# Conv-sequence kernel, second layer: slabs of the forward transform loaded turned by 12 time steps, edge rows taken out of them

## Chip, core and metric

The kernel runs on one core of one Trainium2 chip, in one launch. The metric is the device time of that launch in microseconds (us), as the median of several runs. A profile comes from one execution, with its own time beside it. Engines are called PE (TensorE matmuls), PEld (its weight loads), DVE (VectorE), ACT (ScalarE), POOL (GpSimd) and SP (SyncE, which here only issues DMAs).

## What is computed

The input `x` has shape 4 x 512 x 128 x 64 (batch, time T, nodes, channels), all float32. Layer 0 is a block of a gated recurrence, a convolution along the nodes, a causal convolution in time and a feed-forward part; the change doesn't touch it. Layer 1 splits its input into a moving average over 25 time steps and the rest, and filters the rest in the frequency domain:

```python
left = right = 12            # KERNEL = 25
xpad = concat([first row x left, x, last row x right], axis=time)
c = cumsum(xpad); trend = (c[25:] - c[:-25]) / 25
seasonal = x - trend
xs = rfft(seasonal, axis=time)[:, :128]          # 128 modes
ys = einsum('bmnc,cmk->bknc', xs, w_real + 1j * w_imag)
out = trend + irfft(ys padded to 257, n=512, axis=time)
```

The moving average repeats the first and the last row at the ends. If it wrapped around instead, it would be a circular filter, and the transform of `seasonal` would be one fixed matrix times `x`. The kernel uses that matrix (in `dftv` and `dftd`) and adds a correction that depends on only 24 rows: the first 12 and the last 12 time steps (`dfte` holds its matrix, `HALO` is 12).

## The kernel before

Layer 1 works in `layer1` on two batches at a time. Each pair goes through three stages: `transform` of both batches, `mix`, `invert` of both. So there are two forward transforms in a launch. Layer 0 leaves its result in DRAM as `x4[b]`, time steps by 8192 columns (node and channel).

A slab is all 512 time steps of 512 columns: 128 partitions x 4 blocks of time x 512, 1 MB. There are 16 slabs in a batch. `slab` (L928) loads one with a single DMA from SP into a tile `xin`, tag `big`, of which there are 5 buffers. The weights `w` of the mix use the same 5 buffers (L991), and so do the slabs that `invert` loads again.

`transform` (from L933) takes two slabs at a time, k = 0 and 1; a pair is called a group here, 16 groups in the transform of two batches. In a group, for each k:

- GpSimd issues two DMAs that load 12 rows each, the first and the last time steps, into the tile `edge` (L943, L944; tag `edge`, 2 buffers).
- ACT copies those 24 rows to another place in `edge`, 32 partitions on (L945), since the real and the imaginary part use operands at different partitions.
- DVE forms differences and sums of the blocks of time, `v` (L948) and `u` (L949), and then sums and differences of the halves of `u`, `ev` (L952, two each).

Then PE runs, for both k, the matmuls on `v` (L960), on `ev` (L968) and on `edge` (L977), which accumulate into four PSUM banks, tag a or b in turn. ACT copies the banks to `xf` (L983), the spectrum of the whole batch.

`mix` (L985 on) loads 16 tiles `w` of 1 MB; GpSimd flips the sign of parts of each (L994), PE multiplies (L1001, L1005), and the results go back into `xf`. It starts when `xf` of both batches is there. `invert` forms the inverse transform (L1027 to L1039), loads each slab again together with 6 strips `halo` of 12 rows (L1049, L1052, from SP), adds the moving average on PE (L1055, L1058) and stores `out` (L1062).

The matmuls keep the order in which they are written (`manual_schedule` for PE alone). The order on the other engines is the scheduler's; it puts the loads of later groups ahead of the work of earlier ones as the buffers allow. Each engine runs its instructions, and issues its DMAs, strictly in that order. DMA completions are counted by eight semaphores in turn, so that a DMA waits for the eighth one before it.

Of the kernel before, what the change touches and what calls it, by code (L numbers as in the profile page):

```python
# [10 lines left out]
F32 = mybir.dt.float32  # L11
# [5 lines left out]
P = 128  # L17
T = 512
NF = 128
H = 64  # L20
D = NF * H
NCH = D // P
SL = 512
NS = D // SL
NPR = NCH // 2
NT = T // P
# [4 lines left out]
HALO = KMA // 2  # L31
# [14 lines left out]
def conv_seq_kernel(  # L46
# [27 lines left out]

    layer0(tc, dram, x, xt, vecs, wkvr, wo, wdec, wconv, fbias, w1, fb1, w2, fb2, x4)
    layer1(tc, x4, wri, dftv, dftd, dfte, idfte, idfto, avg, avgh, out)


# [799 lines left out]
def layer1(ctx, tc, x4, wri, dftv, dftd, dfte, idfte, idfto, avg, avgh, out):  # L878
# [7 lines left out]
    nc = tc.nc  # L886
# [4 lines left out]
    dft = ctx.enter_context(tc.tile_pool(name="dft", bufs=1))  # L891
    io = ctx.enter_context(tc.tile_pool(name="io", bufs=2))
# [4 lines left out]
    def load(pool, eng, name, src):  # L897
        t = pool.tile(list(src.shape), F32, name=name)
        eng.dma_start(t, src)
        return t  # L900
# [3 lines left out]
    dfte_sb = load(dft, nc.sync, "dfte_sb", dfte)  # L904
# [5 lines left out]
    def bank(tag):  # L910
        return ps.tile([P, SL], F32, tag=tag, name=tag)


    def by_c(row):
        return row.rearrange("p (a c l) -> p a l c", c=H, l=2)

    def by_n(row):
        return row.rearrange("p (a l c) -> p a l c", c=H, l=2)
# [7 lines left out]
    def slab(b, s):  # L926
        xin = io.tile([P, NT, SL], F32, tag="big", name="xin", bufs=5)
        nc.sync.dma_start(  # L928
            xin, x4[b][:, s * SL : (s + 1) * SL].rearrange("(c p) d -> p c d", p=P)
        )  # L930
        return xin

    def transform(b, xf):  # L933

        for g in range(NS // 2):
            edge = io.tile([P, SL], F32, tag="edge", name="edge")
            uv, ev, pf = [], [], []
            for k in range(2):
                s = 2 * g + k
                c = slice(s * SL, (s + 1) * SL)  # L940
                xin = slab(b, s)
                q = k * H
                nc.gpsimd.dma_start(edge[q : q + HALO, :], x4[b][0:HALO, c])  # L943
                nc.gpsimd.dma_start(edge[q + HALO : q + 2 * HALO, :], x4[b][T - HALO : T, c])  # L944
                nc.scalar.copy(edge[q + 32 : q + 32 + 2 * HALO, :], edge[q : q + 2 * HALO, :])  # L945
                u = io.tile([P, 2, SL], F32, tag="uv0", name="u")
                v = io.tile([P, 2, SL], F32, tag="uv1", name="v")
                nc.vector.tensor_tensor(v, xin[:, 0:2, :], xin[:, 2:4, :], ALU.subtract)  # L948
                nc.vector.tensor_tensor(u, xin[:, 0:2, :], xin[:, 2:4, :], ALU.add)  # L949
                t = io.tile([P, 2, SL], F32, tag="ev", name="ev")  # L950
                for i, op in enumerate((ALU.add, ALU.subtract)):
                    nc.vector.tensor_tensor(t[:, i, :], u[:, 0, :], u[:, 1, :], op)  # L952
                uv.append(v)
                ev.append(t)
                pf.append([bank("ab"[g % 2]), bank("ab"[g % 2])])
            for k in range(2):
                for i in range(2):
                    for r in range(2):
                        h = 1 - r
                        nc.tensor.matmul(  # L960
                            pf[k][r][h * H : (h + 1) * H, :], lhsT=dftd_sb[:, i, r, :], rhs=uv[k][:, i, :],
                            start=(i == 0), stop=False,
                        )
            for k in range(2):
                for i in range(2):
                    for r in range(2):
                        q = r * H + i * H // 2
                        nc.tensor.matmul(  # L968
                            pf[k][r][q : q + H // 2, :], lhsT=dftv_sb[:, i, r, :], rhs=ev[k][:, i, :],
                            start=True, stop=False,  # L970
                        )
            for k in range(2):
                for r in range(2):
                    at = slice(k * H + 32 * r, k * H + 32 * r + 2 * HALO)
                    for h in range(2):
                        hs = slice(h * H, (h + 1) * H)
                        nc.tensor.matmul(  # L977
                            pf[k][r][hs, :], lhsT=dfte_sb[at, hs], rhs=edge[at, :], start=False, stop=True
                        )
            for k in range(2):  # L980
                s = 2 * g + k
                for r in range(2):
                    nc.scalar.copy(by_c(xf[:, r, s * SL : (s + 1) * SL]), by_n(pf[k][r]))  # L983
# [86 lines left out]
    with tc.manual_schedule(engines={nc.tensor.engine}):  # L1070
        for b0 in range(0, B, G):
            xf = spec.tile([P, G, 2, D], F32, tag="xf", name="xf")
            for b in range(G):
                transform(b0 + b, xf[:, b, :, :])
            mix(xf)
            for b in range(G):
                invert(b0 + b, xf[:, b, :, :])


def _constants():  # L1080

    a = np.zeros((T, T))
    for t in range(T):
        for s in range(t - HALO, t + KMA - HALO):
            a[t, min(max(s, 0), T - 1)] += 1.0 / KMA
    around = np.zeros((T, T))
    for t in range(T):
        for s in range(t - HALO, t + KMA - HALO):
            around[t, s % T] += 1.0 / KMA
    k, n = MODES, np.arange(T)  # L1090
    angle = 2.0 * np.pi * ((k[:, None] * n[None, :]) % T) / T
    waves = np.stack([np.cos(angle), -np.sin(angle)])

    dft = waves @ (np.eye(T) - around)
    at = np.concatenate([np.arange(HALO), np.arange(T - HALO, T)])
    edge = (waves @ (around - a))[:, :, at]
    dfte = np.zeros((2, 32, M))
    dfte[0, : 2 * HALO] = edge[0].T
    dfte[1, : 2 * HALO] = np.roll(edge[1], H, axis=0).T
    weight = np.where(k == 0, 1.0, 2.0)[:, None] / T  # L1100
    idft = waves * weight
    idft[1, k == 0] = 0.0
    q = H // 2
    idfte = np.concatenate([idft[r, i : i + q, :P] for i in (0, q) for r in range(2)])
    idfto = np.concatenate([idft[r, H:, : T // 2] for r in range(2)])
    tiles = [slice(i * P, (i + 1) * P) for i in range(NT)]
    avg = np.stack([a[s, s].T for s in tiles], axis=1)
    avgh = np.zeros((NT, 32, P))
    for j, s in enumerate(tiles):
        at = [t for t in range(s.start - HALO, s.start) if t >= 0]  # L1110
        at += [t for t in range(s.stop, s.stop + HALO) if t < T]
        avgh[j, : len(at)] = a[s][:, at].T
    c = {
        "dftv": dft[:, :H, :P].reshape(2, 2, H // 2, P).transpose(3, 1, 0, 2),
        "dftd": dft[:, H:, : T // 2].reshape(2, H, 2, P).transpose(3, 2, 0, 1),
        "dfte": np.concatenate([dfte.reshape(2 * 32, M)] * 2),
        "idfte": idfte,
        "idfto": idfto.reshape(M, 2, P),
        "avg": avg,
        "avgh": avgh.reshape(P, P),  # L1120
    }
    return {n: v.astype(np.float32) for n, v in c.items()}


def _inputs(x, i):
# [22 lines left out]
    for rows, parts in ((MODES, ("w_real", "w_imag")), (IMAG, ("w_imag", "w_real"))):  # L1148
# [16 lines left out]
        "fb2": np.concatenate([i["ffn_b2"]] * 2)[:, None],  # L1165
        "wri": wri.reshape(H, M, 2, 2, M).transpose(1, 0, 2, 3, 4),
        **_constants(),
    }
    return {n: np.ascontiguousarray(v) for n, v in a.items()}
# [17 lines left out]
```

## Time and profile before

| | |
|---|---|
| median of 3 runs | 3746.26 us (3743.07 to 3754.74) |
| the profiled execution | 3747.14 us, its span 3745.2 us |
| busy: PE, DVE, ACT, POOL | 3536.6, 2669.1, 1759.4, 522.6 us |
| DMA | 913.42 MB in 429269 packets, 244 GB/s over the span |
| first transform: first load issued, mix begins | 2757.08, 2891.50 us |
| second transform: third load issued, mix begins | 3246.58, 3376.00 us |

The spans of time are from the start of the profiled span. A line of a timeline gives start, length, engine, source line, operation, output and inputs, the count, and in brackets the idle time of the engine before it with what ended it. A line of the table of stretches gives the length of a stretch, the busy time of PE, PEld, DVE, ACT and POOL in it, the granted clock of PE (1.00 is full), the mean busy share of the core's 16 DMA engines, and what they moved in GB/s. The share can pass 1 a little, since packets overlap.

### The profile page before, as it was taken

The numbers are of one execution on the slowest core, as the hardware profiler recorded it, in microseconds if no ns is written. First come the engines' busy times: TensorE is split into PE (matmuls) and PEld (weight loads), VectorE is DVE, ScalarE is ACT, GpSimd is POOL, SyncE is SP. The second block draws the span as 40 slices with busy tenths as digits, with TensorE's granted clock in tenths as the row PEclk, the third lists the DMA queues.
The fourth block names the chain that finished last, engine by engine and source line by source line (L and its number), as shares of the span: only waits on it lengthen the run. The fifth ranks groups of instructions, "written<-read, shape, count | busy, mean of one in ns | idle before, by whom it ended". The sixth has DMA issues, their size and how long they took to land. (4 is left out here: it accounts for less than half of the span.)

```text
span 3745.2 us, 53017 instructions
## 1 busy us (share of the span) xinstructions
PE 3536.6 (94%) x20041; PEld 1368.8 (37%) x20041; DVE 2669.1 (71%) x3498; ACT 1759.4 (47%) x2299; POOL 522.6 (14%) x782
## 2 busy tenths in 40 slices
PE   9999999999998999999999989999988999989998
PEld 4433322234333223433322233333323843328533
DVE  4445569976776896677789799946667277892677
ACT  0013346655656565565656578868854200142100
POOL 0000012310101121001112122100013000130000
PEclk9999999999999999999999999999999999999999
DMA  9867648787875688788568678645567478993687
GB/s 316 276 206 245 226 163 269 255 280 267 288 263 169 233 279 273 267 292 281 178 231 285 214 248 267 232 152 192 201 233 262 156 235 294 316 322 127 214 285 265
DMA packets 429269, 913.42 MB, mean 244 GB/s; under 512 B 33240, under 2 KB 83672, under 8 KB 424920
## 3 DMA queue, kind: packets, MB, share of 16 engines
q1 hardware_dynamic: 351088, 636.91, 52.4%
q0 software_dynamic: 75776, 271.62, 20.0%
q8 instruction: 160, 2.62, 0.3%
q10 hardware_dynamic: 2152, 1.51, 0.1%
q14 instruction: 93, 0.76, 0.1%
HBM read 641.40 MB, written 268.50 MB: 243 GB/s over the span
## 5 line engine op out<-in xcount | busy, mean ns | idle before, releaser
L744 PE MATMUL p<-mid,w_sb 64*64 64x512 f32 x2048 | 554.8, 599 | 20.2 <-DVE wx L757 20.2
L744 PE MATMUL pb<-mid,w_sb 64*64 64x512 f32 x2048 | 536.7, 599 | 0.0
L736 ACT ACTIVATE mid<-c,fb_sb 128x1024 f32<-128x1024 f32 x256 | 284.6, 1112 | 97.5 <-PE c L731 95.1
L736 ACT ACTIVATE mid<-m,fb_sb 128x1024 f32<-128x1024 f32 x256 | 284.9, 1113 | 93.6 <-PE m L731 92.2
L731 PE MATMUL c<-x,w_sb 64*64 64x512 f32 x2016 | 280.7, 610 | 13.2 <-ACT mid L736 6.9
L731 PE MATMUL m<-x,w_sb 64*64 64x512 f32 x2016 | 283.2, 613 | 6.7 <-ACT ob L776 4.9
L744 PEld LDWEIGHTS p<-mid,w_sb 64*64 64x64 f32 x2048 | 155.5, 135 | 294.8 <-issue 261.6
L408 PE MATMUL a<-xp,wx 128*128 128x512 f32 x512 | 241.7, 615 | 9.1 <-DVE wx L357 8.6
L1032 ACT COPY two<-a 128x512 f32<-128x512 f32 x64 | 37.5, 586 | 428.3 <-PE a L1027 428.3
L1055 PE MATMUL b<-xin,avg_sb 128*128 128x512 f32 x512 | 230.8, 593 | 3.3 <-DVE xin L1061 3.3
L1061 DVE TENSOR_TENSOR xin<-b,pm 128x512 f32<-128x512 f32 x256 | 159.1, 684 | 98.0 <-PE b L1058 83.1
L569 ACT ACTIVATE sq<-x 128x1024 f32<-128x1024 f32 x128 | 135.1, 1055 | 179.4 <-DVE x L566 179.2
L624 DVE SCALAR_TENSOR_TENSOR to<-kd,vec,to 128x510 f32<-128x510 f32 (+1 forms) x272 | 197.2, 745 | 9.9 <-ACT to L620 8.7
L924 DVE COPY xf<-b 128x256 f32<-128x256 f32 x128 | 54.4, 425 | 199.1 <-PE b L1001 179.9
L699 ACT ACTIVATE kd<-kd,vec 128x512 f32<-128x512 f32 x256 | 192.8, 803 | 3.2 <-DVE kd L691 3.2
L251 PE MATMUL st<-x,ones 128*32 128x512 f32 x512 | 173.0, 609 | 12.8 <-DVE x L566 12.8
L624 DVE SCALAR_TENSOR_TENSOR z<-x,vec,z 128x511 f32<-128x511 f32 x240 | 175.9, 745 | 5.3 <-ACT z L620 3.0
L702 DVE TENSOR_TENSOR x<-kd,kx 128x1024 f32<-128x1024 f32 x126 | 154.1, 1223 | 32.6 <-ACT kd L699 32.5
L530 DVE TENSOR_TENSOR x<-a,xp 128x1024 f32<-128x1024 f32 x128 | 156.1, 1220 | 29.1 <-PE a L528 26.9
L528 PE MATMUL a<-rst,wo_sb 64*128 64x512 f32 x512 | 149.2, 657 | 25.1 <-DVE x L530 23.3
L567 POOL DMA_DIRECT2D x<-x x128 | 93.6, 731 | 560.4 <-DVE x L566 544.7
L757 DVE SCALAR_TENSOR_TENSOR x4t<-p,fb_sb,x 128x512 f32<-128x512 f32 x64 | 47.9, 748 | 170.6 <-PE pb L744 168.1
(267 smaller groups left out, 6859.6 us busy)
## 6 DMA issues: line engine op xcount, KB each, us to landing
xp<-in_xt SPq DMA_DIRECT2D x256, 512.0 KB
xin<-x SPq DMA_DIRECT2D x128, 1024.0 KB
kh<-to SPq DMA_DIRECT2D x156, 512.0 KB
x<-x POOLq DMA_DIRECT2D x128, 512.0 KB, 4.6
kx<-x SPq DMA_DIRECT2D x128, 512.0 KB
x<-ob POOLq DMA_DIRECT2D x64, 1024.0 KB, 7.9
out<-xin POOLq DMA_DIRECT2D x64, 1024.0 KB, 6.3
x<-x SPq DMA_DIRECT2D x96, 512.0 KB
```

The lines of the kernel that those rows point to most:

```text
L251: nc.tensor.matmul(st[32 * q : 32 * q + 32, :], lhsT=ones, rhs=src[:, j, :], start=first, stop=last,)
L408: nc.tensor.matmul(pa[:, k, :], lhsT=wq[:, j, k * P : (k + 1) * P], rhs=xp[:, j, :], start=first and j == 0, stop=last and j == 1,)
L528: nc.tensor.matmul(at[:, j, :], lhsT=wo_sb[js, :], rhs=rst[js, :], start=True, stop=True)
L530: nc.vector.tensor_tensor(x1, at, xp, ALU.add)
L624: tap = nc.vector.scalar_tensor_tensor(to[:, j, k:], xr[:, j, : SL - k], vec[:, w, c], to[:, j, k:], ALU.mult, ALU.add)
L699: tc.keep_in_program_order(nc.scalar.activation(d[:, j, :], d[:, j, :], AF.Identity, bias=vec[:, B4, c], scale=vec[:, G4, c]))
L702: nc.vector.tensor_tensor(x3, d, x2, ALU.add)
L731: nc.tensor.matmul(pm[halves[j], h, :], lhsT=w1_sb[halves[h], q * H : (q + 1) * H], rhs=x3[halves[h], j, :], start=True, stop=True,)
L736: nc.scalar.activation(mid, pm, AF.Gelu_apprx_tanh, bias=fb1_sb[:, q : q + 1])
L744: nc.tensor.matmul(sums2[i][j][halves[h], :], lhsT=w2_sb[halves[j], q, :], rhs=mid[halves[j], h, :], start=q == 0, stop=q == 3,)
L1055: nc.tensor.matmul(po[j], lhsT=avg_sb[:, j, :], rhs=xin[:, j, :], start=True, stop=False)
L1061: nc.vector.tensor_tensor(by_n(xin[:, j, :]), by_n(po[j]), by_c(pm[j % 2][:, j // 2, :]), ALU.add)
```

## The change

A new function `shifted_slab` loads the slab turned by 12 time steps: partition p of block c holds time step 128 c + p - 12, modulo 512. It takes three DMAs from SP: 116 rows into partitions 12 to 127 of block 0, the last 12 time steps into partitions 0 to 11 of block 0, and 384 rows into blocks 1 to 3. So partitions 0 to 23 of block 0 hold the 24 edge rows, and GpSimd loads none. ACT copies them from the slab into `edge`: once for k = 0 and twice for k = 1. The fourth place isn't filled; for k = 0 and r = 0 the matmul on the edges reads the slab itself. The matrices are turned to match on the host.

```diff
+    def shifted_slab(b, s):
+        xin = io.tile([P, NT, SL], F32, tag="big", name="xin", bufs=5)
+        c = slice(s * SL, (s + 1) * SL)
+        nc.sync.dma_start(xin[HALO:P, 0, :], x4[b][0 : P - HALO, c])
+        nc.sync.dma_start(xin[0:HALO, 0, :], x4[b][T - HALO : T, c])
+        nc.sync.dma_start(xin[:, 1:NT, :], x4[b][P - HALO : T - HALO, c].rearrange("(c p) d -> p c d", p=P))
+        return xin
...
-                xin = slab(b, s)
-                q = k * H
-                nc.gpsimd.dma_start(edge[q : q + HALO, :], x4[b][0:HALO, c])
-                nc.gpsimd.dma_start(edge[q + HALO : q + 2 * HALO, :], x4[b][T - HALO : T, c])
-                nc.scalar.copy(edge[q + 32 : q + 32 + 2 * HALO, :], edge[q : q + 2 * HALO, :])
+                xin = shifted_slab(b, s)
+                ends = xin[0 : 2 * HALO, 0, :]
+                if k == 0:
+                    first = ends
+                for q in (32,) if k == 0 else (H, H + 32):
+                    nc.scalar.copy(edge[q : q + 2 * HALO, :], ends)
...
-                            pf[k][r][hs, :], lhsT=dfte_sb[at, hs], rhs=edge[at, :], start=False, stop=True
+                            pf[k][r][hs, :], lhsT=dfte_sb[at, hs], rhs=edge[at, :] if k + r else first,
+                            start=False, stop=True,
...
-    at = np.concatenate([np.arange(HALO), np.arange(T - HALO, T)])
+    at = np.concatenate([np.arange(T - HALO, T), np.arange(HALO)])
...
+    dft = np.roll(dft, HALO, axis=2)
```

## Prediction

> **What bounds the kernel now.** Read first the chain of waits in order of time, where it passes through the two forward transforms (times in us from the start of the span, length, what).
>
> ```profile
> 2872.21 1.90 PE a L968 x16
> 2875.39 4.16 DMA w<-in_wri
> 2880.78 5.66 DMA edge<-x
> 2887.82 3.64 ACT xf L983 x7
> ...
> 3354.59 6.57 DMA w<-in_wri
> 3361.19 2.97 issue
> 3365.79 5.15 DMA edge<-x
> 3372.32 3.64 ACT xf L983 x7
> ```
>
> Both transforms end on an edge load, and behind it hangs the mix, which needs all of `xf`. The timeline of GpSimd, ScalarE and TensorE there shows why:
>
> ```profile
> 2870.50 9.79 POOL L994 TENSOR_SCALAR w<-w 128x256 f32<-128x256 f32 x4 [6.62 <-DVE ev L952]
> 2880.24 0.55 POOL L943 DMA_DIRECT2D edge<-x  x1
> ...
> 2886.54 1.25 ACT L945 COPY edge<-edge 24x512 f32<-24x512 f32 x2 [13.83 <-DMA edge<-x]
> ...
> 2879.09 1.92 PE L968 MATMUL b<-ev,dftv_sb 128*32 128x512 f32 x16
> 2886.58 3.24 PE L977 MATMUL b<-edge,dfte_sb 24*64 24x512 f32 x16 [5.56 <-DMA edge<-x]
> 2891.50 1.22 PE L1001 MATMUL b<-xf,w 128*128 128x256 f32 x2 [1.68 <-ACT xf L983]
> ```
>
> The last group's edge loads are issued from GpSimd's queue behind the sign flips of `w` (L994), and TensorE stands 5.56 us. Next the middle of the transform, by the table of stretches (seven us each: busy us of PE, PEld, DVE, ACT, POOL, then granted clock, DMA share, GB/s):
>
> ```profile
> 2770.00:2777.00 7.00, 5.65 (x40) 1.42 (x40) 6.80 (x8) 1.85 (x3) 0.00 (x0) 0.76 1.06 376
> 2805.00:2812.00 7.00, 6.60 (x64) 1.91 (x48) 7.00 (x9) 3.46 (x6) 2.00 (x4) 1.00 1.05 346
> 2847.00:2854.00 7.00, 6.60 (x56) 1.91 (x48) 7.00 (x9) 3.46 (x6) 2.00 (x4) 1.00 0.99 314
> ```
>
> DVE is full, 7.00 of 7.00: a group of two slabs takes its two u, two v and four ev, 2.35 + 2.35 + 2.49 less their overlaps, and comes round every 6.95 us. The DMA engines are nearly full as well: 376 GB/s while the buffers fill, 314 when DVE paces them. Last, the timeline of one group, the queue of SP in it:
>
> ```profile
> 2797.70 2.35 DVE L948 TENSOR_TENSOR v<-xin 128x1024 f32<-128x1024 f32 x2
> 2798.94 0.36 SPq L928 DMA_DIRECT2D xin<-x  x1
> ...
> 2804.50 1.11 PE L977 MATMUL a<-edge,dfte_sb 24*64 24x512 f32 x16
> ...
> 2809.33 2.35 DVE L949 TENSOR_TENSOR u<-xin 128x1024 f32<-128x1024 f32 x2
> ```
>
> The first slab's buffer is free when v has read it (2798.92), and SP refills it at once.
>
> [...] Each transfer leaves a 4-byte packet per engine it used. On SP's queue there are 23,536 in the records of DMA packets; the 1,183 issues other than `halo` in the list of issues, all of 128 partitions, account for 16 each, 18,928; the remaining 4,608 are 384 x 12, so a `halo` load of 12 rows runs on 12 engines. No run shows one of 116 rows. [...] L994 takes 407 ns in the median and 8676 at the longest, in the transform's end.
>
> **The change, part by part.**
>
> The 128 edge loads leave GpSimd's queue (0.50 us each, 64 us of an engine busy 14%). That is worth nothing except at the two ends. There L977 of the last group could start when L968 is done, at 2881.0, and the mix at about 2884.2 in place of 2891.5: 7.3 us. At the second end L968 is done at 3366.0, the mix could start at 3369.2 in place of 3376.0: 6.8. Together **-14 us**. Late next would be nothing: `w` has landed by then.
>
> A slab is now three transfers of 116, 12 and 384 rows of 2 KB. SP issues 64 x 3 in place of 64; at 0.36 us that is 1.1 us a slab, hidden in the 3.5 that a slab has. The bytes of the edges (3.1 MB) go. [...] 116 = 4 x 29 runs on k = 4 engines with 29 rows each, the 12 on twelve with one, the 384 on all with 24. The first four engines carry **29 + 1 + 24 = 54 rows** of each slab, against 32 before; they set when it lands. A row costs, at the 376 GB/s of the full engines, 2048 x 16 / 376 = 87 ns; the shortest packet of 2 KB in the records is 84 ns, and at 346 GB/s it is 95. So a slab takes 54 x 87 = 4.70 us, a group **9.4 us in place of DVE's 6.95**: the bound passes from DVE to four DMA engines. [...]
>
> First transform, from the first issue at 2757.08 to the mix. Now 134.4 us. After: 32 slabs x 4.70 = 150.3; other traffic on those engines at the start, a 1 MB store of `x` (2.8 us per engine) and the 0.56 MB of constants (1.6), 4.4; issue and completion 2.4 (the quickest edge load); from the last landing to the mix 11 (u and v 2.4, L960 3.6, L968 1.9, L977 and the copies of `xf` 3). Sum 168: **+34**. The second: two slabs are loaded early, 30 follow from 3246.58, now 129.4. After: 30 x 4.70 = 141 + two 1 MB stores of `out` 5.6 + 2.4 + 11 = 160: **+31**. In both the 14 us of the ends are already taken off. At 84 ns and without other traffic the sum is +45, at 95 ns +91.
>
> ScalarE copies three times 24x512 in a group, not two: 0.62 us more of an engine busy 3.46 of 7.00; hidden, and if it were not, 32 x 0.62 = 20 us at most. But the copies of group g+2 stand ahead of the `xf` copies of g+1 in its order and now wait for the slabs; at 9.4 us a group these land about when L977 of g+1 ends, which costs 0 to 1 us a group (not added; in the upper end). TensorE does the same matmuls. The one that reads `first` straight from the slab holds its buffer till L977 (2805.2, not 2798.9); DVE needs the refilled one at u of the second next group, 2810.5. That leaves 5.3 us to land where there were 11.5. With 9.4 us a group it leaves over 10, so it costs nothing in the likely case. SP's queue stands longer at that wait; behind it are only slabs and then `w`, whose first is needed 11 us after the last slab.
>
> Nothing else in the kernel is touched. The profiled execution took 3747.1 (span 3745.2), 0.9 over the median of 3746.3. So 3747.1 + 65 = 3812, in terms of the median **3811**.
>
> **Rivals.**
> - Even spread, a gain: the 116 rows go over all sixteen engines, some 8 each, so 33 rows a slab, 2.9 us, and DVE still paces. Then only the two ends remain: -14, 3732. For it: only the 12-row case was seen. [...] an even spread of 12 looks the same, which is the weak point. It decides if a 116-row load puts under 41 rows on its busiest engine (6.95 / 2 / 0.087 = 40, so at most 15 of the 116).
> - The held buffer, no change: an even spread, but 5.3 us to land is too short. From release to release two groups later runs landing L, then 8.6 us (u and v 2.4, L960 and L968 5.5, half of L977 0.7); the pace is (L + 8.6) / 2, above 6.95 once L passes 5.3. A 1 MB store of `out` lands in 6.3 in the median, which gives 7.45, +0.5 x 28 groups = +14 against -14: 3746.
> - The edges were hidden anyway, so nothing changes: against it stand 5.56 us of idle TensorE on the chain.
> - Worse: rows queue on four engines at 95 ns or more, or ScalarE's order adds a us a group: +91 and up, 3840 to 3870.
>
> **How the numbers follow.** Four engines 0.76 (3790 to 3838), worse 0.10, even spread 0.07, held buffer or nothing 0.07. The range 3768 to 3848 takes in the first case whole, with 22 below it, [...] and the lower part of the worse case above it; some 2 in 10 are left out. A measurement here tells 0.3%, 11 us, from no change. Slower 0.86, same 0.07, faster 0.07.
>
> **What would show it.** Right: in the transforms' stretches DVE falls from 7.00 of 7.00 to about 5.2, the DMA share to about (4 x 54 + 12 x 25) / 16 x 87 ns / 4.7 us = 0.6 to 0.65, some 225 GB/s, and DVE and ScalarE wait for `xin`; groups come every 9.1 to 9.7 us; no wait for an edge at the ends. Wrong: groups at 6.95 with DVE full (even spread), or alternating short and long with SP waiting for L977 (held buffer).

## The result and the profile after

| | before | after |
|---|---|---|
| median of 6 runs each | 3743.03 us (3738.35 to 3754.74) | 3843.41 us (3826.54 to 3851.83) |
| ratio, with its 95% interval | | **1.0257 [1.0228, 1.0286]** |
| the profiled execution, its span | 3747.14, 3745.2 us | 3849.67, 3847.9 us |
| first transform, first load issued to mix | 134.4 us | 187.5 us (2764.99 to 2952.54) |
| first mix begins to second mix begins | 484.5 us | 529.6 us (to 3482.14) |
| second mix begins to the end of the span | 369.2 us | 365.7 us |

The kernel is 100 us slower; 3811 was forecast, in a range of 3768 to 3848. In the two profiles the spans differ by 102.7 us. The first transform accounts for 53.1 of it and the stretch from mix to mix, which holds the second transform, for 45.1. The rest, +7.9 ahead of the first load and -3.5 after the second mix began, lies in work that the change doesn't touch; the last section has a likely reason for the -3.5.

The page of the kernel after: its span, the queues of DMA (packets, MB, share) and the chain that ended last.

```profile
span 3847.9 us, 53000 instructions
...
q1 hardware_dynamic: 352112, 636.91, 50.9%
q0 software_dynamic: 71680, 268.46, 19.3%
...
PE 31%; DMA 7%; ACT 3%; issue 3%; DVE 2%; SPq 1%; POOL 0%; ACTq 0%; POOLq 0%; DVEq 0%
DMA xin<-x 6%; PE b L1065 4%; PE p L744 4%; PE b L1011 3%; PE b L1015 3%; PE c L731 3%; PE m L731 3%; PE a L1039 3%; PE b L1068 2%; PE a L1037 1%; PE a L969 1%; DMA halo<-x 1%; ACT z L620 1%; PE m L763 1%; PE c L763 1%
```

The load of a slab now heads the list of what the end waited for, with 6% of the span. SP's queue (q1) holds 1,024 packets more than before (352,112 against 351,088). They are all packets of 4 bytes: 24,560 against 23,536. In the kernel before a load over 128 partitions left 16 of them and one of 12 rows left 12, which is read here as one for each engine that a transfer used; the records don't name engines. There are 16 more for each of 64 slabs. Three transfers on k, 12 and 16 engines leave k + 12 more than the one on 16 did, so **k = 4: the 116 rows run on four engines**.

The chain of waits in the first transform (start, length, what), the kernel after:

```profile
2882.20 15.28 DMA xin<-x
2897.50 12.73 DMA xin<-x
2912.86 6.51 PE a L969 x16
...
2925.47 2.53 SPq L937
2928.05 12.11 DMA xin<-x
2942.75 5.22 PE b L969 x16
2947.97 1.85 PE b L977 x16
```

It goes from load to load. The edge load that stood in it before is gone. DVE's timeline shows the beat of the groups:

```profile
2887.85 1.23 DVE L958 TENSOR_TENSOR u<-xin 128x1024 f32<-128x1024 f32 x1 [3.35 <-DMA xin<-x]
...
2899.69 1.23 DVE L958 TENSOR_TENSOR u<-xin 128x1024 f32<-128x1024 f32 x1 [4.07 <-DMA xin<-x]
...
2910.35 1.23 DVE L958 TENSOR_TENSOR u<-xin 128x1024 f32<-128x1024 f32 x1 [3.62 <-DMA xin<-x]
...
2920.39 1.23 DVE L958 TENSOR_TENSOR u<-xin 128x1024 f32<-128x1024 f32 x1 [3.00 <-DMA xin<-x]
```

DVE stands 3 to 4 us in each group for `xin`, and the groups come 10.0 to 11.8 us apart where they came every 6.95. The table of stretches (length; PE, PEld, DVE, ACT, POOL; granted clock, DMA share, GB/s) for the two transforms after:

```profile
2805.00:2840.00 35.00, 26.93 (x152) 6.68 (x152) 24.77 (x28) 13.24 (x24) 0.00 (x0) 0.86 0.68 202
2840.00:2875.00 35.00, 24.80 (x146) 6.34 (x144) 22.65 (x26) 12.02 (x21) 0.00 (x0) 0.80 0.71 202
2875.00:2910.00 35.00, 25.96 (x180) 7.22 (x176) 21.21 (x24) 13.24 (x23) 0.00 (x0) 0.90 0.68 192
...
3365.00:3400.00 35.00, 30.39 (x192) 8.53 (x190) 25.41 (x30) 13.59 (x24) 0.00 (x0) 0.84 0.69 213
```

DVE is down from full to 21 to 25 of 35 us, and yet the DMA engines are only 0.68 to 0.71 busy in the mean. Neither is full. But a mean over sixteen engines can hide four that are, and the records of DMA packets agree: from 2805 to 2910 us and from 3365 to 3400, 4 or 5 packets are under way at once for 26 to 31% of the time and fewer than 4 for at most 1.4%. The kernel before has 12 or more for 98.7 to 99.9% of its time there (2805 to 2865, 3290 to 3325). Last, the waits (us in total, times, longest):

```profile
ACT edge L954 <- DMA xin<-x: 184.8, 55, 7.3
...
DVE u L958 <- DMA xin<-x: 79.1, 32, 4.3
```

### The profile page after: what moved, and what is told of

Read it like the earlier page. It is cut to its first block, busy times and chain, and to the rows that moved or that the text cites. A ratio compares the mean times of both kernels' runs of the same rounds, so it can differ in the third digit from the quotient of the medians.

```text
span 3847.9 us, 53000 instructions
## 1 busy us (share of the span) xinstructions
PE 3582.1 (93%) x20041; PEld 1378.1 (36%) x20041; DVE 2674.9 (70%) x3498; ACT 1776.7 (46%) x2331; POOL 447.7 (12%) x654
## 3 DMA queue, kind: packets, MB, share of 16 engines
q1 hardware_dynamic: 352112, 636.91, 50.9%
## 5 line engine op out<-in xcount | busy, mean ns | idle before, releaser
L691 DVE TENSOR_TENSOR kd<-kd,rm 128x1024 f32<-128x1024 f32 x128 | 155.9, 1221 | 7.5 <-ACT rm L285 6.0
```

Source lines behind the costliest of these rows:

```text
L691: nc.vector.tensor_tensor(d, d, pair_of(mb), ALU.subtract)
```

## The experiments

Ratios are to the kernel before, on the same chip in the same session (medians of before 3743 to 3746 us); "pace" is the mean distance of two groups on PE, read from the matmuls on `v` over the last seven groups of the first transform and the last twelve of the second.

| run | slab's transfers (rows) | rows on fullest engine | pace, us | median us | ratio [95%] |
|---|---|---|---|---|---|
| before | 512 | 32 | 6.95 | 3743 to 3746 | 1 |
| after | 116, 12, 384, turned by 12 | 54 | 10.0 to 10.5 | 3843.41 | 1.0257 [1.0228, 1.0286] |
| e1_all_copied | as after, no slab held | 54 | 10.5 to 10.7 | 3847.61 | 1.0279 [1.0255, 1.0303] |
| e3_split116 | 116, 12, 384, unturned | 54 | 10.4 to 10.5 | 3873.95 | 1.0348 [1.0327, 1.0368] |
| e6_split118 | 118, 10, 384, unturned | 84 | 14.3 to 14.4 | 3986.98 | 1.0659 [1.0626, 1.0691] |
| e10_cut_112_4 | 112, 4, 12, 384, turned by 12 | 33 | 7.3 to 7.5 | 3743.89 | 0.9994 [0.9981, 1.0006] |
| e2_turn16 | 112, 16, 384, turned by 16 | 32 | 7.5 | 3743.13 | 0.9995 [0.9983, 1.0007] |
| e5_turn16_all_copied | as e2, no slab held | 32 | 7.2 to 7.6 | 3737.97 | 0.9988 [0.9977, 0.9998] |
| e4_split112 | 112, 16, 384, unturned | 32 | 8.1 to 8.3 | 3783.07 | 1.0099 [1.0081, 1.0118] |
| e9_split64 | 64, 64, 384, unturned | 32 | 8.1 to 8.3 | 3792.89 | 1.0132 [1.0115, 1.0149] |
| e7_split128 | 128, 128, 256, unturned | 32 | 6.95 | 3743.57 | 1.0003 [0.9992, 1.0014] |
| e8_copied_edges | 512 | 32 | 6.95 | 3727.02 | 0.9953 [0.9935, 0.9971] |

The unturned splits keep the edge loads of before. The theories: F, the fullest engine sets the pace; H, the slab held for the matmul on the edges does; S, several transfers cost what they cost, whatever their rows.

**e1_all_copied** takes away the held slab alone.

```diff
-                for q in (32,) if k == 0 else (H, H + 32):
+                for q in (k * H, k * H + 32):
...
-                            pf[k][r][hs, :], lhsT=dfte_sb[at, hs], rhs=edge[at, :] if k + r else first,
+                            pf[k][r][hs, :], lhsT=dfte_sb[at, hs], rhs=edge[at, :],
```

> The changed kernel, but all four places of the edge rows are filled by ScalarE (four copies in a group, not three), so that no matmul reads the slab and its buffer is free once v, u and the copies have read it. Theory F (four DMA engines carry 54 rows of each slab): the loads are the same, so 3825 to 3855 us, a group every 10 to 11 us. Rival H (the slab held until L986 leaves too little time for the refill): the time goes back to 3735 to 3775. Rival S (three transfers in place of one, with their issues and semaphores): as F, 3825 to 3855.

Measured 1.0279, with an interval that overlaps the changed kernel's. ScalarE's wait for the slab is what it was (184.8 us before this edit), in the waits of this run:

```profile
ACT edge L954 <- DMA xin<-x: 184.6, 58, 7.7
```

H is out for the changed kernel.

**e2_turn16** keeps all of the change, but turns by 16, so that 112 rows go on sixteen engines (SP's queue holds 353,136 packets, 32 a slab more than before); 32 edge rows take the place of 24, with zero weights for eight of them. `TURN` is 16; the other uses of `HALO` in the loads, copies and matrices of the transform change in the same way.

```diff
-        nc.sync.dma_start(xin[HALO:P, 0, :], x4[b][0 : P - HALO, c])
+        nc.sync.dma_start(xin[TURN:P, 0, :], x4[b][0 : P - TURN, c])
...
-    dft = np.roll(dft, HALO, axis=2)
+    dft = np.roll(dft, TURN, axis=2)
```

> The changed kernel turned by 16 time steps in place of 12: the three transfers have 112, 16 and 384 rows, and 32 partitions of block 0 are the edge operand (8 of them with zero weights). All three divide by 16. F: 7 + 1 + 24 = 32 rows on every engine, as in the kernel before; DVE paces again at 6.95 us a group, and the waits at the two ends are gone: 3725 to 3750. H: the hold of the first slab is still there, so at least half of the loss stays: 3790 or more. S: still three transfers, so 3825 to 3855.

Measured 0.9995: the whole loss is gone. But so are the 14 us that the two ends should have given.

**e3_split116** puts the three transfers alone into the kernel before.

```diff
-                xin = slab(b, s)
+                xin = split_slab(b, s)
...
+        nc.sync.dma_start(xin[0:116, 0, :], x4[b][0:116, c])
+        nc.sync.dma_start(xin[116:P, 0, :], x4[b][116:P, c])
+        nc.sync.dma_start(xin[:, 1:NT, :], x4[b][P:T, c].rearrange("(c p) d -> p c d", p=P))
```

> The kernel before, not turned, with its edge loads, but each slab of the forward transform loaded by three transfers of 116, 12 and 384 rows. F: 54 rows of each slab on four engines, so the transforms slow as in the changed kernel: 3830 to 3865 (the waits for edges at the ends may stay). H: no slab is held, so 3740 to 3755. S: 3830 to 3865.

Measured 1.0348, 9 us above the highest time expected, at the pace of the changed kernel. The three transfers alone make the loss. That it is some 30 us greater fits what stands there beside them: the edge loads, and the waits at the ends, where the mix begins 15.7 and 15.5 us after the last matmuls on `v` (9.8 and 8.2 in the changed kernel). The two ends are 13 of the 30.

**e4_split112** is e3 with 112 in place of 116.

> As the one before, but split into 112, 16 and 384 rows. F: 32 rows on every engine as with one transfer: 3740 to 3760. H: 3740 to 3755. S (three transfers cost, whatever their rows): 3830 to 3865. With the run of 116, 12 and 384 rows beside it, this changes only which engines carry the rows.

Measured 1.0099. Most of e3's loss is gone, and yet 37 us stay with 32 rows on every engine: F does not account for all of it. The table of stretches of this run says where to look (GB/s last):

```profile
2840.00:2875.00 35.00, 31.19 (x222) 8.75 (x226) 29.11 (x33) 13.23 (x24) 8.01 (x16) 0.95 1.07 265
```

All sixteen engines are full now (1.07), at 265 GB/s. Before, they were as full at 314 to 346. So the rows themselves take longer. In the records of DMA packets, rows of 2 KB take 127 to 130 ns in the mean here, 98 in the kernel before.

**e5_turn16_all_copied** is e2 with e1's edit.

> The turned loads by 16 rows (112, 16 and 384 rows, spread evenly over sixteen engines) with all four places of the edge operand copied by ScalarE, so that no matmul on the edges reads the slab and its buffer is free when v and the copies have read it. Theory H for the even case: there the groups come at about 7.2 us, and the slab held until L977 leaves too little time to land; that eats the 14 us of the two ends, and without the hold the time is about 3732 (ratio 0.996). Theory N (a row's place): rows of a 112-row and a 16-row transfer cost more each (112 to 116 ns in the run before, against 97 in the kernel before) with the DMA engines full, so that transfer and not the hold sets the pace: 3740 to 3746 (ratio 0.998 to 1.000), rows again at 110 to 116 ns and the DMA share near 1.00.

Measured 0.9988. The interval leaves out the 0.996 that H gave, and it overlaps e2's: a few us at most belong to the held slab, and whether any do is not settled. Rows take 118 to 120 ns, slow as theory N had them and a little above its 110 to 116; the median lies 2 us below its 3740 to 3746.

**e6_split118** is e3 with 118, to put more rows on fewer engines.

> The kernel before with its edge loads and unturned slabs, the slab loaded as 118, 10 and 384 rows. Theory F (engines used = largest divisor up to 16): 118 = 2 x 59 runs on two engines, 10 on ten, so the busiest two carry 59 + 1 + 24 = 84 rows of a slab, in place of 54 with 116 rows. At the 97 ns a row of the four-engine case a slab takes 8.1 us, a group 16.3 in place of about 10.4 there: 30 groups add about 280 us to the before, some 4025. Every slab leaves 2 + 10 + 16 = 28 completion packets of 4 bytes where an unsplit one leaves 16. Theory S (three transfers cost the same whatever their rows): as with 116 rows, 3874, or as with 112 rows, 3783.

Measured 1.0659. There are 24,304 completion packets of 4 bytes, 12 more a slab than before, as two engines want. DVE's timeline:

```profile
2907.45 1.23 DVE L957 TENSOR_TENSOR u<-xin 128x1024 f32<-128x1024 f32 x1 [5.51 <-DMA xin<-x]
...
2921.49 1.22 DVE L957 TENSOR_TENSOR u<-xin 128x1024 f32<-128x1024 f32 x1 [5.51 <-DMA xin<-x]
...
2935.62 1.23 DVE L957 TENSOR_TENSOR u<-xin 128x1024 f32<-128x1024 f32 x1 [5.54 <-DMA xin<-x]
```

A group every 14.1 us here, 14.3 to 14.4 over the transforms: 2 x 84 rows at 85 ns. The count was right and the price too high: the forecast of +280 took 97 ns, and +243 came. F has passed with a second divisor, and S has failed.

**e7_split128** asks whether e4's 37 us are the price of three DMAs in place of one.

```diff
+        nc.sync.dma_start(xin[:, 0, :], x4[b][0:P, c])
+        nc.sync.dma_start(xin[:, 1, :], x4[b][P : 2 * P, c])
+        nc.sync.dma_start(xin[:, 2:NT, :], x4[b][2 * P : T, c].rearrange("(c p) d -> p c d", p=P))
```

> The kernel before with its edge loads and unturned slabs, the slab loaded by three DMAs of 128, 128 and 256 rows, each over all 128 partitions. It tells apart why 112, 16 and 384 rows, which spread evenly over sixteen engines, still cost 37 us. Theory N (a row's place: a transfer over fewer than 128 partitions gives each engine rows that cost more): nothing is left, 3740 to 3752, rows at about 97 ns as before. Theory L (three DMAs for a slab where eight semaphores count completions in turn, so that fewer slabs are under way, and SP issues three times as much): the 37 us stay, 3775 to 3790, rows as cheap as before or the DMA share below 0.95.

Measured 1.0003, and DVE is full again:

```profile
2830.00:2865.00 35.00, 33.01 (x248) 9.70 (x244) 35.00 (x42) 17.32 (x30) 9.98 (x20) 1.00 0.95 319
```

Here three transfers, with three issues on SP and three turns of the semaphores, cost nothing; each of them goes over all 128 partitions. Rows take 94 ns.

**e9_split64** is e4 with 64 in place of 112; it asks whether two equal pieces cost what 112 and 16 rows do.

> The kernel before with its edge loads, the slab loaded as 64, 64 and 384 rows: all three spread evenly over sixteen engines. It asks why 112, 16 and 384 rows cost 37 us and 128, 128 and 256 nothing. [...] Theory G (any transfer over fewer than 128 partitions makes all rows slow, in it and behind it): as with 112 and 16 rows, three quarters of the rows at 100 to 160 ns, 3775 to 3795.

Measured 1.0132, the same pace as e4, at 258 GB/s:

```profile
2840.00:2875.00 35.00, 29.67 (x194) 8.22 (x196) 29.36 (x34) 14.38 (x26) 7.98 (x16) 0.89 1.06 258
```

In the records 73 to 84% of the rows take 100 to 160 ns and under 10% more than that. The two pieces hold only a quarter of the rows, so those of the 384-row transfer, three quarters of all, are slowed as well. G, which only says what happens, fits.

**e10_cut_112_4** is the changed kernel with its 116-row transfer cut in two.

```diff
-        nc.sync.dma_start(xin[HALO:P, 0, :], x4[b][0 : P - HALO, c])
+        n = P - 16
+        nc.sync.dma_start(xin[HALO : HALO + n, 0, :], x4[b][0:n, c])
+        nc.sync.dma_start(xin[HALO + n : P, 0, :], x4[b][n : P - HALO, c])
```

> The changed kernel with one edit: its transfer of 116 rows is cut into two, 112 rows (7 on each of sixteen engines) and 4 rows (one on each of four), so that a slab is four transfers and the busiest engine carries 7 + 1 + 1 + 24 = 33 rows in place of 54. Everything else of the change stays, the turn by 12 and the slab read by the matmul on the edges too. Theory F (engines used = largest divisor up to 16, and the fullest engine sets the pace): nearly all of the 97 us goes, 3735 to 3755; the rows still cost about 115 ns with the engines full, as with a turn by 16. Theory S (what costs is that a slab is several transfers): 3843 or more. Completion packets a slab: 16 + 4 + 12 + 16 = 48.

Measured 0.9994. Four rows moved into a transfer of their own take away the whole 100 us, though the slab is four transfers now. Completion packets are 25,584, or 32 a slab more than before, as expected. Its two transforms in the table of stretches:

```profile
2830.00:2865.00 35.00, 31.93 (x236) 8.40 (x232) 33.57 (x39) 19.12 (x32) 0.00 (x0) 1.00 1.03 287
3290.00:3325.00 35.00, 31.82 (x236) 8.53 (x235) 34.06 (x40) 19.29 (x33) 0.00 (x0) 1.00 1.03 297
```

DVE is all but full, the DMA engines quite full, at 287 to 297 GB/s with rows at 114 to 120 ns. The pace is 7.34 to 7.45 us, 0.4 to 0.5 over DVE's. By some 15 groups in each transform that is about 13 us, as much as the ends give back (the mix begins 9.1 and 9.2 us after the last matmuls on `v`, in place of 16.0 and 15.5). By this reading that is where the -14 went, here and in e2.

**e8_copied_edges** leaves the slab whole and unturned and copies the edge rows out of it on ScalarE; the matrix of the edges is spread to match on the host.

```diff
-                nc.gpsimd.dma_start(edge[q : q + HALO, :], x4[b][0:HALO, c])
-                nc.gpsimd.dma_start(edge[q + HALO : q + 2 * HALO, :], x4[b][T - HALO : T, c])
-                nc.scalar.copy(edge[q + 32 : q + 32 + 2 * HALO, :], edge[q : q + 2 * HALO, :])
+                nc.scalar.copy(edge[q : q + 32, :], xin[P - 32 : P, NT - 1, :])
+                nc.scalar.copy(edge[q : q + HALO, :], xin[0:HALO, 0, :])
+                nc.scalar.copy(edge[q + 32 : q + H, :], edge[q : q + 32, :])
...
-                    at = slice(k * H + 32 * r, k * H + 32 * r + 2 * HALO)
+                    at = slice(k * H + 32 * r, k * H + 32 * r + 32)
```

> The kernel before with its single 1 MB load of an unturned slab, and no edge loads either: ScalarE builds the 32-row edge operand from the slab with three copies for each k (partitions 96 to 127 of block 3, then partitions 0 to 11 of block 0 over their first rows, then the whole to the second place; eight rows meet zero weights). If the 14 us of the two ends can be had when the loads stay whole, 3732 (ratio 0.996), no wait for an edge at the ends, groups at 6.95 us with DVE full. ScalarE has six copies in a group where before it had two, 2.5 us more of an engine busy 3.46 of 7.00. Rival: its copies delay the xf copies or the ends' idle time was hidden by something else: 3743 to 3750.

Measured **0.9953 [0.9935, 0.9971], 17 us faster than before** and the fastest of all these kernels. PE's timeline at the end of the first transform:

```profile
2864.77 3.65 PE L960 MATMUL b<-v,dftd_sb 128*64 128x512 f32 x16 [0.40 <-DVE v L948]
2868.36 1.92 PE L968 MATMUL b<-ev,dftv_sb 128*32 128x512 f32 x16
2870.21 1.11 PE L977 MATMUL b<-edge,dfte_sb 32*64 32x512 f32 x16
2872.99 0.70 PE L1001 MATMUL b<-xf,w 128*128 128x256 f32 x2 [1.67 <-DMA w<-in_wri]
```

From the last matmuls on `v` to the mix are 8.2 us, where the kernel before had 16.0 (2875.51 to 2891.50). The second end gives the same 8.2 against 15.5. And the middle stays at DVE's pace:

```profile
2830.00:2865.00 35.00, 32.99 (x242) 9.79 (x244) 35.00 (x41) 29.81 (x52) 5.63 (x1) 1.00 0.89 305
```

DVE has 35.00 of 35.00, and ScalarE, at 29.81, hides its six copies.

## Why the prediction was right, and where a size was off

**Four engines for 116 rows: right, and shown.** Ahead of the result no run had such a load, and four was an assumption of the author's. SP's queue holds 16, 12 and 32 packets more a slab than before with 116, 118 and 112 rows, which gives 4, 2 and 16 engines (taking 12, 10 and 16 for the short piece beside them). As far as loads are counted here it is the largest number up to 16 that divides the rows: 64, 128 and 384 have 16 as well, and the 12 of a `halo` load 12. Which of the engines they are, the records don't tell; the sums of 54 and 84 take it that the short transfer runs on the fullest ones too, which is one row of each sum. e10 and e6 move only the count on the fullest engine, 33 and 84, and the time follows both ways. The rival of an even spread falls with it, and e10 shows what an even spread would have brought: 3744 and not the 3732 given for it.

**54 rows at 87 ns, 9.4 us a group: the count was right, the row too cheap.** This is the term that was mis-sized. The last seven groups of the first transform come every 10.48 us (2869.42 to 2942.75), or 97 ns for each of 108 rows. Twelve of the second come every 10.0 (3353.91 to 3473.91), or 93 ns. Both take it that the four engines never pause. On 32 and 30 slabs of 54 rows the difference is 17 and 9 us, 26 of the 33 by which the two stretches (+98) exceed the forecast (+65). The other 7 are not resolved. The 87 ns came from whole transfers over 128 partitions. In the changed kernel some 25 to 40% of the rows take 100 to 160 ns, by the stretch, in the kernel before 12 to 18%. The bound from above, 95 ns and +91, was the better value; the measured interval, +85 to +107, holds it. So the mechanism was the likely one, but 3843 lies above the 3790 to 3838 that it was given with a chance of 0.76. It belongs to the rival "worse", which had 0.10, in its first form: rows at 95 ns or more on four engines. The range holds it with 5 us to spare. (The shortest row of 2 KB in the records is 81 ns, 2% of them; the 84 that the prediction calls the shortest is the most frequent, four in five of those that SP issued. Nothing in the sum rests on it.)

**The ends, -14: right in size, but not to be had at that price.** There is no wait for an edge at the ends of the changed kernel. e8 shows the gain by itself: 7.8 us at the first end and 7.3 at the second, forecast 7.3 and 6.8. "Late next would be nothing" was close: the first mix of e8 waits last for `w`, 1.67 us, as long as the 1.68 that it waited for the copies of `xf` in the kernel before, and loses nothing by it.

**The held slab costs nothing: right**, by e1. For the even spread the rival gave +14, and e2 did come out at no gain as it said; but e5, without the hold, has the slow rows, the same pace in the first transform (7.6 us) and 0.3 us less in the second. The slow rows are the cause that is seen.

**Three issues a slab at 0.36 us, hidden: the size was wrong, the cause is not there.** In e7 an issue takes 0.4 to 0.5 us in the mean, and the three cost nothing. In the changed kernel the issue of 12 rows, behind that of 116, takes as little at the start and about 3 us once loads are under way (L936 issues the 116 rows, L937 the 12, L938 the 384):

```profile
2764.99 0.32 SPq L936 DMA_DIRECT2D xin<-x  x1
2765.37 0.31 SPq L937 DMA_DIRECT2D xin<-x  x1
2765.72 0.39 SPq L938 DMA_DIRECT2D xin<-x  x1
...
2791.63 1.76 SPq L936 DMA_DIRECT2D xin<-x  x1
2793.44 3.32 SPq L937 DMA_DIRECT2D xin<-x  x1
2796.80 0.38 SPq L938 DMA_DIRECT2D xin<-x  x1
```

The three issues take 2.8 us a slab in its first transform in place of 1.1, 4.1 to 4.3 in e1 and e3 and 6.4 to 6.5 in e6, of the 7.1 to 7.2 that a slab has there. So a pace set by SP's issues is a rival. Against it stand e10, with four issues a slab at 0.3 to 0.4 us in the mean, and the second transform of the changed kernel, where SP has time to spare (it waits up to 5.4 us for DVE to free a buffer) at a pace of 10.0. The long issues look like a wait for the full engines, longer with more rows on them; where the wait stands, no run shows.

**ScalarE's third copy is hidden: right**; even six copies are in e8. Whether its order adds up to 1 us a group, as the upper bound had it, no run isolates.

**The signs named in advance.** DVE's share came out at 4.2 to 5.1 of 7, forecast 5.2; DMA share 0.68 to 0.71 and 192 to 213 GB/s against 0.60 to 0.65 and 225. Fewer GB/s follow from the slower pace, 10.0 to 10.5 us and above the 9.1 to 9.7 that were named. The higher share doesn't: if all rows grew dearer alike it would stay where it was. It takes rows on the other twelve engines that are dearer still. If the four are full, shares of 0.69 and 0.71 leave 115 to 130 ns for each of the 50 rows of a group there, by my estimate; the mean over all rows in the records is 105 to 114 ns.

**What stays open.** Why a transfer over fewer than 128 partitions slows the rows, those of full transfers among them, is not settled. Rows of 100 to 160 ns are about 5% of all with two full engines (e6), some 25 to 40% with four, and 46 to 91% with sixteen that carry such pieces (e2, e4, e5, e9, e10). That would fit engines that hinder each other; whether they do, and where, no run shows. Nor is it settled why e4 is slower than e2, 8.1 to 8.3 us a group against 7.5 with the same 112, 16 and 384 rows: the edge loads and the partitions of the pieces both differ.

## What to carry to other kernels

Before a load is cut, write down for each piece how many engines it runs on (in the loads here the largest divisor of its rows up to 16: 4 for 116, 2 for 118, 16 for 112), add up the rows on the fullest engine, and price that engine, not the mean: the mean DMA share of 0.7 with consumers waiting was four full engines here. Spread evenly is not yet as good as whole: with pieces over fewer than 128 partitions a row took 112 to 130 ns (e2, e4, e5, e10) against 94 to 98 with whole ones (e7, before), so a few rows needed elsewhere were cheaper to copy from the slab on an engine that had time (e8) than to place by the load. A wait that shows only at the ends of a stage is worth its few us only if the remedy leaves the beat of the middle alone.

## What the runs showed of the hardware that was not expected

Transfers of 112 and 16 or of 64 and 64 rows, all on sixteen engines, moved 258 to 272 GB/s with the engines full and the edge loads beside them (e4, e9), and 278 to 297 without (e2, e5, e10), where whole ones moved 314 to 346. Edge loads may do a little of the same: rows of up to 85 ns are 41 to 53% of all in the kernel before (by stretches of 35 us up to 65%) and 63 to 78% in e8, which has none.

The granted clock of PE, which the prediction left out, moves with the waits. Its records show only 0.5 and 1.00 in the transforms, 0.5 for 3.4, 6.8, 10.2 or 13.7 us. In the first transform of the changed kernel the drops follow stretches of 3.4 us in which PE was busy for 0 to 1.8 us; two others with 1.7 and 1.8 us (from 2812.8 and 2877.7) have none behind them, so the trace doesn't show what decides. With waits of 1.6 to 6.1 us there the mean is 0.80 to 0.90, and the matmuls on `v` take up to 6.5 us in place of 3.65, which hides in the wait for the slabs. At the start of the mix, after the 5.56 us of the edge wait, the kernel before has 0.69 for eight us:

```profile
2892.00:2900.00 8.00, 8.00 (x27) 6.44 (x27) 0.85 (x2) 0.75 (x2) 0.00 (x0) 0.69 0.04 11
```

and e8, which comes there without a wait, has the full clock:

```profile
2873.00:2881.00 8.00, 8.00 (x36) 6.74 (x37) 1.70 (x4) 1.74 (x5) 0.77 (x2) 1.00 0.07 19
```

By 8 x 0.31 that is some 2.5 us of PE's work at that end beside the wait itself. The records have the kernel before at 0.5 for 13.7 us from 2883.4 and again from 3368.1, at the second end, and e8 nowhere between 2764.6 and 3235.7. So by estimate the clock is worth about 5 us at the two ends together, and it is a likely reason why the stretch after the second mix began is 2.5 us shorter in e8 and 3.5 in the changed kernel: in all twelve profiles that stretch goes with the time at 0.5 in it, 364.3 to 366.9 us with 7 to 11 us of it and 368.6 to 370.2 with 16 to 17. With the 15.1 us of the waits that makes 20 for e8, where 17 were measured (11 to 24 by the interval); this is read from the trace, and no run took it apart.
